# Idle TensorE products at the seams of a two-stage kernel, and one projection step to a tile

## The chip, the cores and the metric

The kernel runs on one core of a Trainium2 chip. The metric is the device time of one execution in microseconds (us). All data are float32. The core has five queues that work side by side: TensorE (PE) for matrix products, VectorE (DVE), ScalarE (ACT), GpSimd (POOL) and SyncE (SP), which here only starts transfers. A matrix product writes to PSUM, from where VectorE or ScalarE takes it. PEld is the loading of TensorE's stationary operand.

## The reference

Two computations follow each other. The first is a bidirectional recurrence over 4 batches, 1024 steps and 1024 channels: with a decay d per channel, `a[t] = a[t-1] * d + exp(k[t]) * v[t]` and `b[t] = b[t-1] * d + exp(k[t])`, forward and backward; the result x is `sigmoid(r)` times the ratio of the two sums, times a gain per batch.

The second repeats a block twice (NB = 2) on x, with S = 16 slots, K = 4 and 16 heads:

- `logits = rms(x) @ compete_w.T + compete_b`; for each slot the best four rows, with softmax weights
- `written` = the weighted sum of those four rows of `x @ write_w.T + write_b`; `ws = rms(ws + written)`
- q from x, keys and values from ws; attention of each row over the 16 slots; `x = rms(x + ctx @ out_proj_w.T + out_proj_b)`

The output is the input x plus the result.

## The kernel before

**Recurrence (to about 413 us).** The channels lie on partitions, so 32 tiles (i = 0 to 31: four batches, eight tiles of 128 channels) of 128 x 1024 are worked through, one per turn of a Python loop. Everything is emitted in a fixed program order (`pin` keeps an instruction in its place on its engine), and work on tile i is interleaved with the ends of tiles i - 1 and i - 2. VectorE does four scans per tile (`both`, L315), and three elementwise operations. ScalarE does the exponentials, one sigmoid over four tiles each time i % 4 is 0 (HK = 4; L274, with a table load before and behind it), the copies of transposed tiles, and the small `edges` values (L327) that the backward scans begin with. TensorE adds terms (`num`, L365), contracts a tile into the first block's logits (`raw`, L437), and transposes tiles (`ptr`, L451) to rows, which ScalarE sends to memory (`rows`).

Between these the loop places the steps of the list `projection`. They prepare `wo_cw`, the product of the output weights with the slots' competition weights, which the first block needs to get the second block's logits. `turn_weights(j, h)` transposes half of one 128-row tile of the output weights on TensorE (`pwt`, L483) and copies it back with ScalarE (L484); `group_products(j)` multiplies it in groups of four channel tiles (`acc`, L490, copied at L498); `group_sums` adds the groups (`pc`, L504, L508). There are 8 x 3 + 1 = 25 steps. All of them, and the transposes of tiles, share one PSUM bank, `ptr`, so each step waits for the copy of the one before.

SP issues the loads in program order: `kf` (the tile to come), `gate`, the output weights `wp` in four pieces from i = 2 on, write weights and key and value weights ahead of the first block (`load_ahead`), and the stores `turned_rows`. The pieces of weights share nine buffers (`wide`), so key and value pieces 1 to 4 take those of `wp` and wait for `group_sums`.

**Seam 1 (about 413 to 467 us).** After the last tile, its halves are finished, the logits are normalised, the last two tiles are transposed (`turn_ptr`, `turn_columns`, `turn`, L692) and copied out (L698). Then `write_slots(blk)` begins: VectorE finds each slot's four best rows; TensorE brings their numbers into two columns (`token_ps`, L769), GpSimd gathers the rows (L779), a second such product brings the weights (`share_ps`); then `pmix` (L807) forms the weighted sums, `pw` (L825) multiplies by the write weights, `pkv` (L875) by key and value weights, `pk` and `pv` fold the query and output weights into maps.

**Attention (twice 32 tiles of 128 rows).** `run` does, per tile, `psc` (scores, L1085), softmax, `pet` (transposes), `po` (output, L1142) and the norm. In the first block it also makes the second block's logits: `poc` (L1158), scaled, transposed by `turn_logits` (`lg`, L1227). Seam 2 (about 762 to 791 us) lies between the blocks: the last `lg`, top four, token, gather, the transposes of the first two row tiles (`ptr`, L1073, in `early`), `pmix` and `pw`.

## Time and profile before

| what | us |
|---|---|
| three timed runs | 1104.65, 1105.7, 1109.95 (median 1105.7) |
| the profiled execution | 1103.67, of which the span is 1101.9 |
| recurrence: one step, VectorE without a wait | 12.44 |
| first seam: pmix, pw | 7.06, 9.29 |
| second seam: pmix, pw | 3.84, 7.09 |
| mean granted clock of TensorE over the span | 0.945 of full |

The profile's page gives the busy share of each engine in 40 slices of the span (27.5 us each), the TensorE clock that was granted, and the chain of work that ended last. A timeline row reads: start, duration, engine, line and operation, what it writes and reads, the shape, how many, and in brackets the idle time of its engine before it and what ended it. Lines are those of the kernel before.

### The profile page before, as it was taken

The numbers are of one execution on the slowest core, as the hardware profiler recorded it, in microseconds if no ns is written. First come the engines' busy times: TensorE is split into PE (matmuls) and PEld (weight loads), VectorE is DVE, ScalarE is ACT, GpSimd is POOL, SyncE is SP. The second block draws the span as 40 slices with busy tenths as digits, with TensorE's granted clock in tenths as the row PEclk, the third lists the DMA queues.
The fourth block names the chain that finished last, engine by engine and source line by source line (L and its number), as shares of the span: only waits on it lengthen the run. The fifth ranks groups of instructions, "written<-read, shape, count | busy, mean of one in ns | idle before, by whom it ended". The sixth has DMA issues, their size and how long they took to land.

```text
span 1101.9 us, 11887 instructions
## 1 busy us (share of the span) xinstructions
PE 961.6 (87%) x4116; PEld 538.3 (49%) x4116; DVE 767.3 (70%) x1049; ACT 508.8 (46%) x791; POOL 546.3 (50%) x417
## 2 busy tenths in 40 slices
PE   2678787887878785899999999996899999999996
PEld 0223232322323232584666666664584676676763
DVE  7999999999999995144666666666234556555555
ACT  5475858667686753012344444444113333333332
POOL 4999889998999972100222222222100443434444
PEclk9798888999889898799999999999999999999999
DMA  8485564857564374590487778562770455555554
GB/s 270 144 295 157 168 188 138 277 160 248 153 214 132 93 243 114 204 396 21 172 294 261 262 259 294 183 222 92 282 285 21 160 192 197 196 196 205 191 210 153
DMA packets 121787, 218.78 MB, mean 199 GB/s; under 512 B 10928, under 2 KB 76592, under 8 KB 121728
## 3 DMA queue, kind: packets, MB, share of 16 engines
q1 hardware_dynamic: 87872, 199.15, 51.0%
q10 hardware_dynamic: 33280, 16.78, 5.3%
q0 software_dynamic: 576, 2.10, 0.6%
q8 instruction: 32, 0.52, 0.2%
q14 instruction: 27, 0.22, 0.1%
HBM read 150.90 MB, written 67.11 MB: 198 GB/s over the span
## 4 chain that ended last, share of the span: by engine, by line
PE 60%; DVE 24%; issue 5%; ACT 4%; POOL 3%; DMA 3%; SPq 1%; POOLq 0%; DVEq 0%; ACTq 0%
PE psc L1085 20%; PE po L1142 19%; DVE both L315 17%; DVE both L414 3%; PE pk L945 3%; PE pkv L875 3%; PE raw L437 2%; PE ptr L1073 2%; DVE ov L359 2%; PE pv L1013 2%; PE num L365 2%; PE pw L825 1%; PE pet L1131 1%; PE pmix L807 1%; PE poc L1158 1%
## 5 line engine op out<-in xcount | busy, mean ns | idle before, releaser
L1085 PE MATMUL psc<-km,xt 128*128 128x272 f32 (+1 forms) x1024 | 238.4, 386 | 0.0
L1142 PE MATMUL po<-vm,e 128*128 128x512 f32 x512 | 230.4, 593 | 0.9 <-ACT e L1132 0.9
L1085 PEld LDWEIGHTS psc<-km,xt 128*128 128x128 f32 x1024 | 189.5, 190 | 29.1
L365 PE MATMUL num<-ov,minus_ident 128*128 128x512 f32 x128 | 87.6, 821 | 96.1 <-DVE ov L359 96.1
L1119 POOL TENSOR_TENSOR e<-e,den 128x256 f32<-128x256 f32 x64 | 40.5, 633 | 253.7 <-DVE den L1117 232.2
L315 DVE TENSOR_TENSOR_SCAN both<-columns,edges,both 128x1024 f32<-128x1024 f32 x64 | 148.4, 2319 | 2.8 <-ACT edges L327 2.8
L1142 PEld LDWEIGHTS po<-vm,e 128*128 128x128 f32 x512 | 94.8, 190 | 95.7 <-issue 85.4
L1183 DVE SCALAR_TENSOR_TENSOR y<-y,inv,npost_bc 128x1024 f32<-128x1024 f32 x62 | 79.7, 1285 | 41.2 <-POOL inv L1178 41.2
L1151 DVE TENSOR_TENSOR y<-po,y 128x512 f32<-128x512 f32 x128 | 85.8, 674 | 30.4 <-PE po L1142 30.1
L1171 ACT ACTIVATE junk<-y 128x1024 f32<-128x1024 f32 x63 | 66.7, 1059 | 69.2 <-DVE y L1183 69.1
L365 PEld LDWEIGHTS num<-ov,minus_ident 128*128 128x128 f32 x128 | 27.6, 239 | 132.8 <-issue 68.4
L407 POOL TENSOR_TENSOR both<-both,quo 128x1024 f32<-128x1024 f32 (+1 forms) x33 | 75.7, 2293 | 20.4 <-ACT quo L394 19.7
L1178 POOL TENSOR_TENSOR inv<-mean,minus_half 128x1 f32<-128x1 f32 x64 | 35.5, 555 | 96.0 <-DVE mean L1176 96.0
L303 POOL TENSOR_TENSOR ekv<-ek,kf 128x1024 f32<-128x1024 f32 (+1 forms) x33 | 75.6, 2292 | 2.6
L1132 ACT COPY e<-pet 128x256 f32<-128x256 f32 x64 | 23.8, 372 | 112.8 <-PE pet L1131 112.7
L408 POOL TENSOR_TENSOR gate<-gate,quo 128x1024 f32<-128x1024 f32 (+1 forms) x33 | 75.4, 2284 | 0.0
L1280 POOL TENSOR_TENSOR y<-y,xin 128x1024 f32<-128x1024 f32 x31 | 73.2, 2361 | 1.4 <-DVE y L1183 1.4
L426 POOL TENSOR_TENSOR gate<-gate,both 128x1024 f32<-128x1024 f32 x31 | 73.3, 2363 | 1.2
L315 DVE TENSOR_TENSOR_SCAN both<-columns,ek 128x1024 f32<-128x1024 f32 (+1 forms) x32 | 71.5, 2234 | 2.4 <-POOL gate L426 2.4
L437 PE MATMUL raw<-gate,lhs 128*32 128x512 f32 x128 | 71.2, 681 | 0.6 <-POOL gate L426 0.6
L315 DVE TENSOR_TENSOR_SCAN both<-columns,ekv 128x1024 f32<-128x1024 f32 (+1 forms) x32 | 71.5, 2233 | 0.0
L1176 DVE TENSOR_SCALAR mean<-total 128x1 f32<-128x1 f32 x64 | 9.9, 154 | 85.4 <-ACT junk L1171 46.0
(195 smaller groups left out, 1522.5 us busy)
## 6 DMA issues: line engine op xcount, KB each, us to landing
y<-rows SPq DMA_DIRECT2D x64, 512.0 KB, 4.2
kf<-in_ft_dram SPq DMA_DIRECT2D x32, 512.0 KB, 5.2
gate<-in_xt_dram SPq DMA_DIRECT2D x32, 512.0 KB, 6.5
turned_rows<-gate SPq DMA_DIRECT2D x32, 512.0 KB, 3.5
xt<-turned_rows SPq DMA_DIRECT2D x32, 512.0 KB, 5.1
rows<-y SPq DMA_DIRECT2D x32, 512.0 KB, 3.0
xin<-in_x_dram SPq DMA_DIRECT2D x32, 512.0 KB, 4.5
rows<-stage ACTq DMA_DIRECT2D x31, 512.0 KB, 3.3
```

Source lines behind the costliest of these rows:

```text
L303: pin(nc.gpsimd.tensor_tensor(ekv[:, part], ek[:, part], kf[:, part], ALU.mult))
L315: nc.vector.tensor_tensor_scan(dst[:, way], dec, src[:, way], start, ALU.mult, ALU.add)
L365: nc.tensor.matmul(num_ps[:, ts(h, 512)], minus_ident, src[:, ts(h, 512)], start=first, stop=not first,)
L407: pin(nc.gpsimd.tensor_tensor(den, den, quo[:, part], ALU.mult))
L408: pin(nc.gpsimd.tensor_tensor(xk, xk, quo[:, part], ALU.mult))
L426: pin(engine.tensor_tensor(xk, xk, factor[:, part], ALU.mult))
L437: nc.tensor.matmul(raw[rows_b, ts(h, 512)], lhs[:, w].rearrange("p h s -> p (h s)"), src[:, ts(h, 512)], start=(k == 0 and w == k), stop=( ...
L1085: nc.tensor.matmul(psc[g][:, :n], xt_g[g][:, k, :], maps["km"][:, g // NT, k, :n], start=(k == 0), stop=(k == NK - 1),)
L1142: nc.tensor.matmul(po, et[:, ts(c, P)], vm[:, c, ts(h, 512)], start=(c == 0), stop=(c == 1),)
L1151: pin(nc.vector.tensor_add(half, po, half))
L1183: pin(nc.vector.scalar_tensor_tensor(y[g], y[g], inv[g], npost_bc, ALU.mult, ALU.mult))
L1280: pin(nc.gpsimd.tensor_add(y[g - 1], y[g - 1], xin[g - 1]))
```

## The change

It adds a helper, `hold_clock(bank, n)`, which emits n products of the identity with the first 512 columns of `npost_bc`, a constant, into a PSUM bank that nobody reads. They are placed: 7 behind the last copies of the recurrence (in the bank `ptr`), 5 in the first block and 1 in the second ahead of `pmix` (behind `early`), 4 in the first block's last turn behind `turn_logits` of the last tile but one, and 3 at the start of the second block's top four, ahead of token.

It also changes the projection. `group_products` now does two 128-row tiles in one step, with 16 products and one copy, so there are 16 + 4 + 1 = 21 steps in place of 25. One is taken in every tile with i % 4 not 0, from i = 3 on; before, it was 0, 1, 1, 2 for i % 4 = 0 to 3, from i = 5 on. The last is taken at i = 30 (before: 29). The four loads of `wp` are issued at i = 1 to 4 in place of 2 to 5, and of the last four loads of key and value weights, two each at i = 30 and 31 before, all stand at i = 31.

```diff
+    def hold_clock(bank, n):
+
+        for _ in range(n):
+            pin(nc.tensor.matmul(bank, ident, npost_bc[:, :512], start=True, stop=True))
...
-        def group_products(j):
-            acc = rec_ps.tile([P, 4, P], F32, tag="ptr", bufs=1, name=f"acc_{j}")[:, 0, :]
-            for o in (0, 2, 4, 6, 1, 3, 5, 7):
-                pin(
-                    nc.tensor.matmul(
-                        acc[ts(o // 2, 2 * S), :],
-                        cw_pad[:, o, :],
-                        weight_rows(j)[:, ts(o, P)],
-                        start=(o % 2 == 0),
-                        stop=(o % 2 == 1),
-                    )
-                )
-            pin(nc.scalar.copy(weight_rows(j)[:, :P], acc))
+        def group_products(j2):
+            acc = rec_ps.tile([P, 4, P], F32, tag="ptr", bufs=1, name=f"acc_{j2}")
+            for n in range(2):
+                for o in (0, 2, 4, 6, 1, 3, 5, 7):
+                    pin(
+                        nc.tensor.matmul(
+                            acc[ts(o // 2, 2 * S), n, :],
+                            cw_pad[:, o, :],
+                            weight_rows(2 * j2 + n)[:, ts(o, P)],
+                            start=(o % 2 == 0),
+                            stop=(o % 2 == 1),
+                        )
+                    )
+            pin(nc.scalar.copy(wo_next[j2][:, :, :P], acc[:, :2, :]))
...
-        for j in range(NJ):
-            for h in range(2):
-                projection.append(lambda j=j, h=h: turn_weights(j, h))
-            projection.append(lambda j=j: group_products(j))
+        for j2 in range(NJ // 2):
+            for n in range(4):
+                projection.append(lambda j=2 * j2 + n // 2, h=n % 2: turn_weights(j, h))
+            projection.append(lambda j2=j2: group_products(j2))
...
-            if 2 <= i < 6:
-                wo_next.append(load_rows(wo, i - 2, f"wp{i - 2}"))
+            if 1 <= i < 5:
+                wo_next.append(load_rows(wo, i - 1, f"wp{i - 1}"))
...
-            if i >= N - 2:
-                for n in range(2):
-                    load_ahead(0, 5 + 2 * (i - N + 2) + n)
+            if i == N - 1:
+                for n in range(5, 9):
+                    load_ahead(0, n)
...
-            for _ in range(min((0, 1, 1, 2)[i % HK], len(projection)) if i > HK else 0):
+            if i >= 3 and i % HK and projection:
                 projection.pop(0)()
...
             send(j, stage)
+        hold_clock(rec_ps.tile([P, 512], F32, tag="ptr", bufs=1, name="idle"), 7)
     rc_stack.close()
...
+        if last:
+            hold_clock(bank("po", "idle_topk"), 3)
         token = small_tile([P, 2], "token", U32)
...
         early()
+        hold_clock(bank("po", f"idle_rows{blk}"), 5 if first else 1)
...
                     turn_logits(g - 1)
+                    if here and not next_:
+                        hold_clock(bank("po", "idle_norm"), 4)
```

## The prediction

> **What bounds the kernel now.** I read the page's 40 slices first, then the chain in order of time, then TensorE's timeline at the two seams, the granted clock by stretches, and VectorE's idle times in the recurrence.

> ```profile
> PE 2678787887878785899999999996899999999996
> DVE  7999999999999995144666666666234556555555
> PEclk9798888999889898799999999999999999999999
> ```

> Three stages. Up to 413 us VectorE is full and steps follow each other every 12.44 us: only what makes VectorE wait counts there. From 467 us on, apart from the stretch around slice 28, TensorE is full at full clock. Between lie two seams in which neither is full; at the first (slices 15 to 17) the clock is low as well. TensorE's timeline there:

> ```profile
> 428.75 1.04 PE L692 MATMUL turn<-ident,gate 128*128 128x128 f32 x8
> 436.86 0.38 PE L769 MATMUL token_ps<-at,pick 128*64 128x2 f32 x4 [7.07 <-DVE neg L758]
> 437.99 0.38 PE L769 MATMUL share_ps<-wgt,pick 128*64 128x2 f32 x4 [0.75 <-DVE wgt L787]
> 443.76 7.06 PE L807 MATMUL pmix<-spare,spare 128*128 128x64 f32 x32 [5.40 <-DMA spare<-in_wb_dram]
> 451.28 9.29 PE L825 MATMUL pw<-ww,mix_t 128*64 128x512 f32 x32 [0.46 <-ACT mix_t L815]
> ```

> and at the second seam, between the blocks, the same work:

> ```profile
> 762.03 0.51 PE L1158 MATMUL poc<-vmc,e 128*128 128x16 f32 x4
> 764.02 0.28 PE L1227 MATMUL lg<-ident,lgs 128*16 128x128 f32 x1 [1.47 <-DVE lgs L1216]
> 768.36 0.38 PE L1227 MATMUL lg<-ident,lgs 128*16 128x128 f32 x1 [4.07 <-DVE lgs L1216]
> 772.04 0.38 PE L769 MATMUL token_ps<-at,pick 128*64 128x2 f32 x4 [3.30 <-DVE neg L758]
> 773.66 3.43 PE L1073 MATMUL ptr<-ident,y 128*128 128x128 f32 x16 [0.17 <-DMA y<-rows]
> 777.54 3.84 PE L807 MATMUL pmix<-spare,spare 128*128 128x64 f32 x32 [0.46 <-DMA spare<-rows,token]
> 781.85 7.09 PE L825 MATMUL pw<-ww,mix_t 128*64 128x512 f32 x32 [0.46 <-ACT mix_t L815]
> ```

> Equal products, 16.35 us at the first seam and 10.93 at the second; both stand on the chain. The clock says why (columns: stretch, its length, then busy us of PE, PEld, DVE, ACT, POOL, and the granted clock):

> ```profile
> 66.63:70.04 3.41, 1.51 (x4) 0.22 (x2) 3.38 (x3) 3.41 (x1) 3.33 (x3) 1.00 1.03 423
> 428.45:431.85 3.40, 1.33 (x13) 1.10 (x11) 3.15 (x6) 2.91 (x5) 0.00 (x0) 1.00 0.01 2
> 431.87:443.70 11.83, 0.76 (x8) 0.65 (x8) 5.58 (x15) 1.46 (x4) 4.97 (x6) 0.50 0.68 193
> 443.76:450.80 7.04, 7.04 (x32) 6.87 (x32) 0.00 (x0) 0.00 (x0) 0.00 (x0) 0.50 0.15 54
> 773.20:776.60 3.40, 3.23 (x18) 2.79 (x19) 0.45 (x2) 1.17 (x2) 3.10 (x4) 0.50 1.00 367
> ```

> The clock changes on a grid of 3.41 us in this trace. A stretch in which TensorE was busy 1.33 us (0.39) is followed by half clock; after one of 1.51 us (0.44) it stayed. It rose after 3.23 us of transposes (773.2 to 776.6), so the second seam reached pmix at full clock, and at the first seam only after a full stretch of pw: pmix, busy without a break for 7 us, did not raise it. At full clock 128x512 records follow each other at 0.43 us (eight po records in 3.43 us of the chain), so one 128x512 f32 product, two records, is 0.86 us, and 1.71 at half clock.

> In the recurrence VectorE waited four times for ScalarE's edge values, in two of the steps that hold the sigmoid:

> ```profile
> 117.59 2.35 DVE L315 TENSOR_TENSOR_SCAN both<-columns,edges,both 128x1024 f32<-128x1024 f32 x1 [0.62 <-ACT edges L327]
> 124.13 2.35 DVE L315 TENSOR_TENSOR_SCAN both<-columns,edges,both 128x1024 f32<-128x1024 f32 x1 [0.60 <-ACT edges L327]
> 169.24 2.35 DVE L315 TENSOR_TENSOR_SCAN both<-columns,edges,both 128x1024 f32<-128x1024 f32 x1 [1.01 <-ACT edges L327]
> 175.78 2.35 DVE L315 TENSOR_TENSOR_SCAN both<-columns,edges,both 128x1024 f32<-128x1024 f32 x1 [0.60 <-ACT edges L327]
> ```

> 2.83 us in all. The chain leads back from each pair through ScalarE's queue to two projection steps taken one after the other (i = 7 and 11), behind products that ran at half clock.

> **First seam: 7 + 5 idle products.** The 7 write the bank of turn_ptr, so they wait for ScalarE's copy of it (430.80 + 0.57), start at 431.4 and take 7 x 0.86 = 6.0 us, to 437.4. TensorE's token product behind them was ready at 436.86 and also waits for the last of them: +0.6 us. Behind token stand the cast, GpSimd's gather issue (438.40) and, 5.2 us later, pmix: take the 0.6 in full. The slots and bias loads on SP wait for the transposes, not for the idle products, and keep their time. The 5 (4.3 us) follow share at 439.0 and end at 443.3, before the gather's landing (443.76 + 0.6): cost nothing; without that cover each would cost 0.86. Gain: the gap in which the clock fell is now 1.6 us (429.8 to 431.4), so any 3.41 us there hold about 1.8 us of products (0.53, above 0.44): the clock stays. pmix becomes 3.84 (-3.2) and pw 7.09 (-2.2), as at the second seam; the gather's second half landed 2.1 us after the first, no later than a 3.84 us pmix needs it (1.9). Sum: -5.4 + 0.6 = **-4.8 us**. The weight loads behind pw are released by pw itself and move with it.

> [...]

> **Second seam: 4 + 3 + 1 products.** The 4 follow the lg transpose at 764.3 and end at 767.7, before 768.36; the 3 run 768.75 to 771.3, before token at 772.04; the one stands behind the row transposes, ahead of pmix. At full clock all are hidden. These transposes take 2.1 us instead of 3.43, but pmix waits for the gather (777.41), so nothing is won on the profiled execution. If a grid stretch spans the pause of 771.3 to 773.7 the clock falls once more and the last product ends up to 0.8 us after the gather. Between 0 and +0.8: **+0.3**, as that takes about half of the grid's positions. [...] The trace shows 1.00 after 3.4 us of transposes, so I count nothing; but other executions, whose grid lies otherwise, may well start pmix cold. [...]

> **Recurrence: 21 steps.** Removed: the second step in each i % 4 = 3, and eight groups of acc products with eight copies (four of double width take their place). At i = 7 an acc (0.73 of TensorE) and its copy (0.27) leave the queue ahead of the sigmoid: -1.1 of 1.22. At i = 11 a turn (0.60) and its copy (0.59): -1.2 of 1.61. Step i = 3 gets a turn that was not there (0.66 + 0.59): at i = 16, behind two steps, VectorE did not wait, so free. A double group is about 1.2 us of TensorE, no more than a turn with its copy. group_sums (1.96 us) moves from i = 29 to 30, into TensorE's pause of 2.36 us before 400.26; its copy (0.27) precedes a quo that waits until 400.34 anyway. SP: the four output-weight loads go one step earlier, the first ahead of the store at 37.77 into SP's pause from 25 us; two of the four key/value loads move behind the store of i = 29, to 403 us, and behind group_sums. They are done by about 414 us, pkv reads them at 462, and the row stores start at 431.9: free. No POOL instruction moves. **-2.2**, between -2.8 and +2: the grid decides in which steps TensorE is late.

> Sum: -4.8 + 0.3 - 2.2 = -6.7 on the profiled execution (1103.67 us, of which the span is 1101.9): **1097.0 us**. That execution is 2.0 below the median of the runs (1105.7), so against the median it is -8.7, or 0.8%.

> **Rivals.** A: the clock holds over the idle products and falls in pmix, because the 0.8 us pause before it plus a pmix that counts half fall into one stretch. For: pmix did not raise the clock. Against: the second seam's pmix followed a 0.46 us pause without a fall. It costs about 3 us (half of pmix and of one stretch of pw): 1100.0. B: the clock falls before the 7 products, they start cold for up to two stretches (four at 1.71), end at 440.8, and token is 3.9 late: net -1.5 at the seam, 1100.3; with the recurrence unimproved 1102.5. C, slower: the idle products do not raise or hold the clock at all. Then 7 take 12 us (token +6.6), 5 take 8.6 and end 9.8 us after pmix's old start; 4 and 3 at the second seam hold token up by 4.6 more, and the seams gain nothing: 1103.7 + 14.4 - 2.2 = 1115.9. It decides from the second cold product on token's path (0.6 + 2 x 0.86 exceeds the 2.2 of the recurrence). Against: one stretch of pw, with the same 512 columns, raised the clock at 455.7. D: the change does not do what it says: the clock holds but pmix waits for the gather or its loads, and only the recurrence changes: -2.2 + 0.6 + 0.3 gives 1102.4. Against: pmix ran in 3.84 us at the second seam with its gather landing 1.9 us apart.

> **Numbers.** Main 0.63 (1094.5 to 1099.5), A 0.17, B 0.12, C 0.04, D 0.04. Range 1094.0 to 1103.0 leaves out C and B's tail. 0.5%, about what a measurement of this kernel can tell from no change, is 5.5 us: faster below 1100.2. Main and 0.11 of A and B, which end at about that bound, give 0.74, C 0.04, the rest 0.22.

> **What would show it.** Right: granted clock 1.00 from 425 us on through pmix and pw; pmix 3.8 and pw 7.1 at both seams; token at 437.5 or less than 0.7 later than before relative to the transposes; VectorE's waits for edges under 1.5 us in total. Wrong: 0.50 within 431 to 455 us, an idle product longer than 0.86 us apart, or new VectorE waits in the steps i = 4, 8, 12.

## The result, and the profile after

The changed kernel takes 1097.2 us in the median of five runs (1096.5 to 1097.7), beside 1105.2 us of the kernel before: ratio 0.9919, 95% interval 0.9898 to 0.994. Run again beside the experiments it gave 0.9923 (0.9901 to 0.9945). Its profiled execution has 1097.41 us, a span of 1095.6, against 1101.9 before: 6.3 us less. A gain of 8 us in the medians was forecast as 8.7, and 6.3 in the profiled executions as 6.7. The sum holds. Of its three terms, the experiments below bear out the first, contradict the second and leave the third open.

First the 40 slices of the changed kernel:

```profile
PE   2688788877878788899999999998999999999996
DVE  7999999999999995144666666656144555555555
PEclk9789899989989899999999999999999999999999
```

Nothing below 9 is left in the clock from slice 16 on. At the first seam (slices 15 to 17) TensorE is warm, that is, at full clock. At the second (slices 28 and 29) one cold stretch of 3.4 us hides within slice 29; it is shown below. TensorE's timeline at the first seam:

```profile
429.29 6.28 PE L115 MATMUL idle<-npost_bc,ident 128*128 128x512 f32 x14 [1.63 <-ACT stage L704]
435.67 0.28 PE L776 MATMUL token_ps<-at,pick 128*64 128x2 f32 x4
436.92 4.56 PE L115 MATMUL idle_rows<-npost_bc,ident 128*128 128x512 f32 x10
443.23 3.76 PE L817 MATMUL pmix<-spare,spare 128*128 128x64 f32 x32 [1.75 <-POOL bias_rows L808]
447.45 7.09 PE L835 MATMUL pw<-ww,mix_t 128*64 128x512 f32 x32 [0.46 <-ACT mix_t L825]
```

pmix and pw are 10.85 us in place of 16.35. Token has lost its wait for VectorE (7.07 us before): it now stands directly behind the 7 products, which end last. At the second seam:

```profile
757.81 3.60 PE L115 MATMUL idle_norm<-npost_bc,ident 128*128 128x512 f32 x8
762.14 2.74 PE L115 MATMUL idle_topk<-npost_bc,ident 128*128 128x512 f32 x6
765.61 0.28 PE L776 MATMUL token_ps<-at,pick 128*64 128x2 f32 x4 [0.73 <-DVE neg L765]
766.86 3.30 PE L1083 MATMUL ptr<-ident,y 128*128 128x128 f32 x16
771.36 3.76 PE L817 MATMUL pmix<-spare,spare 128*128 128x64 f32 x32
775.58 7.09 PE L835 MATMUL pw<-ww,mix_t 128*64 128x512 f32 x32 [0.46 <-ACT mix_t L825]
```

Here pmix and pw are as long as they were in the profile before. Token to pmix is 5.75 us against 5.50: the +0.3 of the forecast. The 3 products end before token is ready (it waits 0.73 us for neg), so they are hidden. The 4 and the 3 do not keep the clock up, though (columns as in the forecast: stretch, length, busy us of PE, PEld, DVE, ACT, POOL, clock, DMA share, GB/s):

```profile
763.99:767.41 3.42, 1.94 (x16) 1.04 (x15) 2.54 (x9) 0.39 (x2) 1.02 (x1) 1.00 0.93 351
767.41:770.82 3.41, 3.41 (x15) 2.52 (x13) 0.05 (x2) 2.34 (x4) 2.82 (x4) 0.50 0.99 356
```

After a stretch that was busy for 0.57 the clock is at half for one stretch, in which the row transposes run (3.30 us, and not the 2.1 of the forecast). They and the one product behind them fill it (3.41 us), and the clock is at 1.00 again from 770.82 us on, ahead of pmix at 771.36.

In VectorE's waits of the recurrence the edges (2.8 us before) are gone. One wait has grown, at the end of the recurrence, and the stretch of granted clock beside it says why. The wait before, then after:

```profile
418.03 0.76 DVE L414 SCALAR_TENSOR_TENSOR num<-both,twice_root,num 128x512 f32<-128x512 f32 x1 [2.54 <-POOL both L407]
415.90 0.76 DVE L419 SCALAR_TENSOR_TENSOR num<-both,twice_root,num 128x512 f32<-128x512 f32 x1 [3.99 <-PE num L370]
```

```profile
405.59:409.01 3.42, 0.61 (x2) 0.00 (x0) 3.39 (x4) 0.89 (x2) 1.63 (x2) 1.00 1.02 387
409.01:412.42 3.41, 2.96 (x4) 1.41 (x5) 2.87 (x3) 2.91 (x4) 3.41 (x3) 0.50 1.05 402
439.73:443.14 3.41, 1.75 (x5) 0.44 (x3) 0.00 (x0) 0.00 (x0) 2.62 (x4) 1.00 0.98 308
443.14:446.55 3.41, 3.32 (x30) 3.35 (x31) 0.00 (x0) 0.00 (x0) 0.00 (x0) 1.00 0.06 24
```

TensorE had 0.61 us of work in one stretch and ran its last numerator at half clock in the next: VectorE waits 3.99 us there instead of 2.54. The last two lines are the seam: 1.75 us of idle products, then pmix, all at 1.00.

The difference of the two profiled executions, by the end of the turn transposes, the start of pmix and the start of pkv:

| part | before | after | difference | forecast |
|---|---|---|---|---|
| recurrence, to the last turn transpose | 429.79 | 427.66 | -2.1 | -2.2 |
| from there to token | 7.07 | 8.01 | +0.9 | +0.6 |
| token to pmix | 6.90 | 7.56 | +0.7 | 0 |
| pmix to pkv (first seam) | 18.78 | 13.27 | -5.5 | -5.4 |
| token to pmix (second seam) | 5.50 | 5.75 | +0.25 | +0.3 |

The rows add to -5.8 of the 6.3 us. From this table alone the forecast looks right in kind at every term. It compares one execution with one.

### The profile page after: what moved, and what is told of

Its sections match the earlier page's. It is cut to its first block, busy times and chain, and to the rows that moved or that the text cites. A ratio compares the mean times of both kernels' runs of the same rounds, so it can differ in the third digit from the quotient of the medians.

```text
span 1095.6 us, 11962 instructions
## 1 busy us (share of the span) xinstructions
PE 972.7 (89%) x4156; PEld 541.9 (49%) x4156; DVE 767.0 (70%) x1049; ACT 507.5 (46%) x787; POOL 546.4 (50%) x417
## 4 chain that ended last, share of the span: by engine, by line
PE 58%; DVE 31%; issue 4%; POOL 3%; ACT 2%; DMA 1%; SPq 0%; POOLq 0%; DVEq 0%; ACTq 0%
DVE both L320 22%; PE psc L1095 20%; PE po L1152 19%; DVE both L419 3%; DVE ov L364 3%; PE ptr L1083 3%; PE pk L955 3%; PE pkv L885 3%; PE pv L1023 2%; PE pet L1141 1%; PE pw L835 1%; PE raw L442 1%; PE poc L1168 1%; PE num L370 1%; PE pmix L817 1%
```

## The experiments

All ratios are to the kernel before, timed on the same chip beside the kernel in question; its medians there were 1107.5, 1106.5 and 1106.4 us. One thousandth is 1.1 us.

**Either half alone.** The first kernel is the changed one with all `hold_clock` calls taken out:

```
-        hold_clock(rec_ps.tile([P, 512], F32, tag="ptr", bufs=1, name="idle"), 7)
...
-            hold_clock(bank("po", "idle_topk"), 3)
...
-        hold_clock(bank("po", f"idle_rows{blk}"), 5 if first else 1)
...
-                        hold_clock(bank("po", "idle_norm"), 4)
```

> The changed kernel with none of the idle products: only the 21 projection steps and the moved weight loads. Theory: the two halves of the change add up, and this half brings the recurrence's 2.1 us alone (turn transposes end at 427.7 instead of 429.8), while the clock falls at both places as before: pmix 7.0 and pw 9.3 at the first seam, so about 1102 to 1103.5, ratio 0.998. Rival 1: the steps bring most of the 8 us, by moving the stretches in which the clock is judged so that it no longer falls: then about 1098, with pmix 3.8 at the first seam. Rival 2: the saving of the steps is lost again in the last stage's cold stretch: 1105, no change.

Measured: 1105.9 us, ratio 0.9994 (0.9978 to 1.001): -0.7 us, between -2.4 and +1.1. Its profile shows no wait for edges and pmix at 7.06 us.

The second has the idle products at all places and the 25 steps and weight loads of the kernel before (the cut is against the changed kernel, and leaves out `group_products` and the loads at i = 30 and 31):

```
-            if i >= 3 and i % HK and projection:
+            for _ in range(min((0, 1, 1, 2)[i % HK], len(projection)) if i > HK else 0):
                 projection.pop(0)()
...
-            if 1 <= i < 5:
-                wo_next.append(load_rows(wo, i - 1, f"wp{i - 1}"))
+            if 2 <= i < 6:
+                wo_next.append(load_rows(wo, i - 2, f"wp{i - 2}"))
```

> The kernel before with the idle products at all their places (7, 5, 4, 3, 1) and its own 25 projection steps and loads. Theory: -5.5 from pmix and pw, +1.6 for the later token and gather, +0.3 at the second seam: -3.6 to -4.2, about 1101, with pmix 3.8 and pw 7.1 at the first seam and VectorE's four waits for edges (2.8 us) still there. Rival 1 (the products bring nothing alone): 1105. Rival 2 (they bring nearly all, since the steps' saving would be hidden behind the seam): 1098.

Measured: 1096.9 us, ratio 0.9923 (0.9902 to 0.9943), as much as the whole change. Rival 2 is right about the size: the idle products carry all of the gain that can be measured. Its reason, that the steps' saving would be hidden, was not tested. Nor did the waits for edges come back with the 25 steps. In this profile only three steps are longer than the 12.44 us of the others, by about 0.2 us each, against 2.83 us in the profile before. In the changed kernel's second profile, with 21 steps, one wait of 0.41 us stands. So those waits differ from execution to execution: the profile before showed an execution with many. In the twelve profiles with 21 steps they come to 0.9 us at most in any one; only two profiles have 25 steps, one with 2.8 us and one with none.

**The change again.** The changed kernel was timed once more beside the kernels that follow.

> The changed kernel itself, beside these. Theory: its times lie close together (within 1.5 us), since both seams are warm in every execution, and 8 to 10 us below the kernel before, whose executions spread over 7 us. Rival: its spread is that of the kernel before, with a median near 1099.

Measured: 1098.5 us (1095.4 to 1099.9), ratio 0.9923 (0.9901 to 0.9945). The difference holds; the forecast of its spread does not, 4.5 us instead of 1.5. The kernel before, beside it, spread from 1100.8 to 1111.8. So the change has taken away a part of what differs between executions, not all.

**Either seam alone.** The changed kernel without the 4, 3 and 1:

```
-        if last:
-            hold_clock(bank("po", "idle_topk"), 3)
...
-        hold_clock(bank("po", f"idle_rows{blk}"), 5 if first else 1)
+        if first:
+            hold_clock(bank("po", f"idle_rows{blk}"), 5)
...
-                    if here and not next_:
-                        hold_clock(bank("po", "idle_norm"), 4)
```

> The changed kernel without the 4, 3 and 1 products at the second seam; the 7 and 5 at the first stay. Theory: they are hidden and bought nothing on the profiled grid: TensorE falls to half clock near 764 to 767 us in both, the row transposes then run 3.4 us at half clock and raise the clock before pmix; 1097 within 0.7, ratio to the changed kernel 1.000. Rival (insurance: the grid of the clock lies otherwise from run to run or after the earlier changes): pmix starts at half clock and pmix and pw take 16.3 instead of 10.9 us: about 1102.

Measured: 1101.0 us (1097.0 to 1107.5), ratio 0.9949 (0.9928 to 0.997). Its profiled execution took 1107.54 us, and its second seam (timeline) shows what the profile before did not:

```profile
776.87 7.06 PE L816 MATMUL pmix<-spare,spare 128*128 128x64 f32 x32 [0.96 <-DMA spare<-rows,token]
784.39 8.39 PE L834 MATMUL pw<-ww,mix_t 128*64 128x512 f32 x32 [0.46 <-ACT mix_t L824]
```

15.45 us in place of 10.85. The row transposes ran here too, at half clock, but the stretch in which most of them fell held 2.50 us of work (0.73), and the clock did not rise. The insurance rival is right: without products the second seam was warm in one execution and cold in another, and the grid of stretches lay otherwise in the two: the transposes began 0.46 us after the start of a stretch in the profile before (773.66 and 773.20), and 1.26 us ahead of one here (772.15 and 773.41). Of the three profiles without them, two reached pmix warm after 10.2 us at half clock (the kernel before and the steps alone) and this one stayed cold for 23.9 us. In the eleven profiles with the 4, 3 and 1 the cold part is one stretch of 3.4 us in ten, with pmix warm in each (3.68 to 3.94 us), and two stretches in one. Which of the 4, the 3 and the 1 earns this was not tested.

This execution is long for a second reason. It lost the clock at the first seam as well, with the 7 and the 5 in place:

```profile
441.99 6.76 PE L816 MATMUL pmix<-spare,spare 128*128 128x64 f32 x32 [1.98 <-issue]
449.21 8.73 PE L834 MATMUL pw<-ww,mix_t 128*64 128x512 f32 x32 [0.46 <-ACT mix_t L824]
```

Here pmix began 1.98 us after the end of the 5, and pmix and pw lost 4.6 us, as much as at the second seam. So of the 10.1 us between this execution and that of the profile after, the two seams hold 9.2, in equal parts.

And the changed kernel without the 7 and the 5:

```
-        hold_clock(rec_ps.tile([P, 512], F32, tag="ptr", bufs=1, name="idle"), 7)
...
-        hold_clock(bank("po", f"idle_rows{blk}"), 5 if first else 1)
+        if last:
+            hold_clock(bank("po", f"idle_rows{blk}"), 1)
```

> The changed kernel without the 7 and the 5 products; the 4, 3 and 1 at the second seam stay. Theory now: each seam's products are worth what its cold pmix and pw cost where they are cold, and the two add: the first seam -5.5 +1.5 = -4, the second 0 to -5.5 by the execution, in the median -3 to -4; so 4 us above the changed kernel, about 1101 to 1102, with pmix 7.0 and pw 9.3 at the first seam. Rival: the first seam's cold clock is hidden behind the weight loads after it (wkv, wq) and its products bring less than 1.5: 1098.

Measured: 1102.8 us, ratio 0.9971 (0.9957 to 0.9985), pmix 7.06 and pw 8.82 at the first seam. Against the changed kernel (0.9921, the mean of its two ratios) the first seam's products are worth 0.0050, 5.5 us (3 to 8, if the intervals of the ratios are combined), and the second seam's 0.0028, 3.1 us (0 to 6). Together that is 8.6 of the whole's 8.7: they add, and the middle values leave nothing for the steps.

**Which products of the first seam.** Without the 7, and without the 5:

```
only_five:   -        hold_clock(rec_ps.tile([P, 512], F32, tag="ptr", bufs=1, name="idle"), 7)
only_seven:  -        hold_clock(bank("po", f"idle_rows{blk}"), 5 if first else 1)
             +        if last:
             +            hold_clock(bank("po", f"idle_rows{blk}"), 1)
```

> The changed kernel without the 7 products at the end of the recurrence; the 5 ahead of pmix stay. Theory A (the 5 alone warm the clock): token comes 0.9 us earlier, the 5 start at half clock (1.7 us each) and the clock rises after one or two stretches of 3.4 us, so they end within 1 us of the gathered rows; pmix and pw at full clock or nearly: 1096 to 1098. Theory B (7 are needed): the 5 are still at half clock when they end, pmix does not raise it, and the seam is as without products, with 2 us of the 5 on top: 1102 to 1104.

> The changed kernel without the 5 products ahead of pmix; the 7 stay. Theory: TensorE then stands still for 7 us between share and pmix, the clock falls there, pmix 7.0 and pw 9.3 as before and the token is 0.9 us late on top: 1101.5 to 1103, worse than without both. Rival: the clock holds from the 7 through the pause: 1097.

Measured: with the 5 alone 1098.4 us, ratio 0.9929 (0.9907 to 0.9951), the same as the whole change; with the 7 alone 1103.3, ratio 0.9972 (0.9954 to 0.999), as without either, with pmix at 7.06. The five alone, in the timeline and by stretches:

```profile
434.59 6.23 PE L115 MATMUL idle_rows<-npost_bc,ident 128*128 128x512 f32 x10
440.65 3.99 PE L816 MATMUL pmix<-spare,spare 128*128 128x64 f32 x32
```

```profile
434.57:437.98 3.41, 3.41 (x6) 1.52 (x5) 0.42 (x2) 0.00 (x0) 2.99 (x3) 0.50 0.61 169
437.98:441.40 3.42, 3.42 (x15) 1.89 (x13) 0.00 (x0) 0.00 (x0) 1.97 (x4) 1.00 0.87 280
```

They start at half clock, fill one stretch, and the clock is at 1.00 in the next. Token stands 7.07 us behind the transposes again, as before the change. The 7 hold a clock that the 5 bring back here anyway, and cost token 0.9 us. This execution's grid suits the five exactly, and it is the fastest of its six; that they always warm in time isn't shown (the runs reach from 1095.3 to 1099.8).

**Five in place of seven.**

```
-        hold_clock(rec_ps.tile([P, 512], F32, tag="ptr", bufs=1, name="idle"), 7)
+        hold_clock(rec_ps.tile([P, 512], F32, tag="ptr", bufs=1, name="idle"), 5)
```

> The changed kernel with 5 products instead of 7 at the end of the recurrence (they end 1.7 us earlier, at 433.9 instead of 435.6; token's input is ready at 434.7). Theory: token starts 0.9 us earlier and everything behind it too, if the pause between the 5 and token (0.9 us) does not let the clock fall: -0.9, about 1096.3. Rival 1: pmix starts when its gathered rows land, and they land late since they share the DMA queues with the slots and wb loads, which keep their time: no more than -0.3, about 1097. Rival 2: the pause makes the clock fall at token: pmix at half clock, up to +5.4, 1102.6.

Measured: 1097.5 us (1096.0 to 1101.1), ratio 0.9918 (0.9897 to 0.9938), the same as the change. Token is back at 7.08 us behind the transposes and pmix 7.07 behind token, so the 0.9 us is the products' doing. That the rows land late because they share queues with the other loads isn't borne out: token to pmix is 6.7 to 7.8 us in all profiles but that of the narrow products below, early token or late. In its profiled execution (1101.09 us) rival A of the prediction happened: pmix took 4.90 us and pw 9.26, 3.3 us more than warm (the forecast said 3). The stretch ahead of the fall:

```profile
442.77:446.19 3.42, 2.86 (x24) 2.79 (x25) 0.00 (x0) 0.00 (x0) 0.18 (x1) 1.00 0.43 139
```

TensorE was busy for 0.84 of it, all with pmix's products of 64 columns, and the clock fell to 0.50 in the next. That led to the next test.

**Busy time, or columns.** The five products of 512 columns become 38 of 64:

```
-            pin(nc.tensor.matmul(bank, ident, npost_bc[:, :512], start=True, stop=True))
+            pin(nc.tensor.matmul(bank[:, :c], ident, npost_bc[:, :c], start=True, stop=True))
...
-        hold_clock(bank("po", f"idle_rows{blk}"), 5 if first else 1)
+        if first:
+            hold_clock(bank("po", "idle_rows0"), 38, 64)
+        else:
+            hold_clock(bank("po", f"idle_rows{blk}"), 1)
```

> The changed kernel with the 5 products of 512 columns ahead of pmix replaced by 38 of 64 columns, which keep TensorE busy for about as long (pmix needs 0.117 us each: 4.5 us). Theory: what holds the clock is the columns that pass, not the busy time: these count as pmix does, half or less, the clock falls before pmix, which then takes 7.0 us and pw over 8: 1101.5 to 1103, as without the 5. Rival: busy time holds it: 1097 to 1098.5, pmix 3.8.

Measured: 1102.2 us (1098.0 to 1110.9), ratio 0.9973 (0.9947 to 0.9999). The time is no clean answer, since the products were mis-sized: each is two records, 0.11 us apiece at full clock, so 38 would keep TensorE busy for 8.5 us and not 4.5, and hold pmix up by themselves. The twelve executions fall into two groups, eight from 1098.0 to 1102.6 us and four from 1109.9 to 1110.9. The profiled one (1110.7 us) is one of the four:

```profile
436.40 13.98 PE L115 MATMUL idle_rows<-npost_bc,ident 128*128 128x64 f32 x76
```

```profile
435.75:439.16 3.41, 2.98 (x29) 2.99 (x29) 0.71 (x4) 0.00 (x0) 2.28 (x3) 1.00 0.48 112
442.58:445.99 3.41, 3.41 (x18) 3.41 (x17) 0.00 (x0) 0.00 (x0) 0.00 (x0) 0.50 0.05 19
445.99:449.40 3.41, 3.41 (x18) 3.41 (x17) 0.00 (x0) 0.00 (x0) 0.00 (x0) 0.50 0.00 0
```

After a stretch that was busy to 0.87 the clock fell, and in the following stretches, busy without a break, it stayed at 0.50 (to 452.82 us), and pmix behind them took 7.04 us. So narrow products did not raise the clock here. Whether they held it went with how many fell into the stretch: here 25 began in the one ahead of the fall, while pmix's, 30 in a stretch, held it alone in the changed kernel (443.14 to 446.55). The eight faster executions have no profile; probably the clock held in them.

**Toward a better version.** Three more products in TensorE's pause ahead of the last numerator; 6 and 7 in place of 7 and 5 at the first seam; and both of these with one more product ahead of the 16-column pboc products in the first block, behind which the clock fell for a stretch in the second profile of the changed kernel (it followed 492.3 to 495.7 us, in which TensorE was busy for 0.81; pv after it took 1.7 us longer):

```
tail_three:  +            if i == N - 1:
             +                hold_clock(rec_ps.tile([P, 512], F32, tag="ptr", bufs=1, name="idle_last"), 3)
                          add_negated(num_ps[i], ov, True)
six_seven:   -        hold_clock(rec_ps.tile([P, 512], F32, tag="ptr", bufs=1, name="idle"), 7)
             +        hold_clock(rec_ps.tile([P, 512], F32, tag="ptr", bufs=1, name="idle"), 6)
             -        hold_clock(bank("po", f"idle_rows{blk}"), 5 if first else 1)
             +        hold_clock(bank("po", f"idle_rows{blk}"), 7 if first else 1)
all_three:   both, and
                                  pb = bank("aux", "pboc", 1)
             +                    hold_clock(pb, 1)
```

> The changed kernel with 3 more products in TensorE's pause ahead of the last numerator (405.9 to 409.4 us). Theory: where the clock falls at about 409 (the changed kernel's profile: VectorE then waits 3.99 us for the last num in place of 2.54), it no longer does: -1.4 in those executions, about -0.7 to -1 in the median: 1096.5 to 1097.5, and the wait is 2.5 in the profile. Rival: the wait is set by VectorE's and GpSimd's own work: no change, 1098.

> The changed kernel with 6 products in place of 7 at the end of the recurrence and 7 in place of 5 ahead of pmix. Theory: token starts 0.6 to 0.8 us earlier, and the longer row ahead of pmix leaves no pause in which the clock could fall: -0.7 in the median and no pmix over 4 us: 1097 to 1097.8. Rival: the 7 end after the gathered rows have landed and hold pmix up by what token won: 1098.3.

> The changed kernel with the two edits above (3 products ahead of the last numerator; 6 and 7 at the first seam) and one more product ahead of the 16-column pboc products, behind which the clock fell for one stretch in some executions (pv 4.95 instead of 3.27 us). Theory: these are the places where executions still differ; the three bring 0.8 + 0.7 + (0.8 - 0.3) = 2 us in the median and leave a spread under 2 us: about 1096. Rival: one product there costs 0.9 on a full TensorE and the others bring nothing: 1098.5 to 1099.

Measured: 1099.8 us, ratio 0.9946 (0.9927 to 0.9965), for the three at the tail. They did not help. In this execution TensorE's last raw products ended 1.4 us later than in the changed kernel's profile (407.6 against 406.2), and the idle ones were still running when the last ov was ready:

```profile
407.56 2.84 PE L115 MATMUL idle_last<-npost_bc,ident 128*128 128x512 f32 x6
410.24 1.88 PE L370 MATMUL num<-ov,minus_ident 128*128 128x512 f32 x4
```

VectorE then waited 3.35 us for num, better than 3.99 but worse than the 2.54 of executions whose clock holds anyway. In the profile of all three together the same products cost nothing (2.54). An idle product is free only in a pause that is always there.

Six and seven gave 1097.0 us (1095.2 to 1098.5), ratio 0.9915 (0.9898 to 0.9933): as fast as the change, with the lowest ratio of all, but the intervals overlap, so no gain over it is shown. Its profile has the shortest span of all (1093.4 us), with token 0.85 us nearer to the transposes than in the change and pmix at 3.79. All three together gave 1097.7 (1095.4 to 1103.6), ratio 0.993 (0.9904 to 0.9956): no gain, and the spread is not gone. Its profile shows where the spread still comes from, at the second seam:

```profile
766.97:770.38 3.41, 2.29 (x18) 1.77 (x16) 0.00 (x0) 0.32 (x1) 0.39 (x1) 1.00 0.48 183
```

```profile
768.64 5.47 PE L819 MATMUL pmix<-spare,spare 128*128 128x64 f32 x32 [1.12 <-DMA spare<-rows,token]
```

Here the gathered rows came 1.1 us after the one product ahead of pmix was done. That pause and the beginning of pmix fell into one stretch (busy 0.67), and the clock fell in pmix. More products at that place weren't tried, nor was six and seven with the single product ahead of pboc alone.

## Why the prediction was right, and where it was not

**The total** was right: 1097.0 forecast, 1097.2 measured. That it came so close is in part luck. The forecast for the profiled execution, -6.7, was set against the median of the runs, which gave another -2.0 that no term explains. A gain at the second seam, which the forecast put at +0.3, and a recurrence that brings less than the -2.2 then cancelled.

**First seam, -4.8.** Right in kind and nearly in size. In the profile pmix and pw brought 5.5, as forecast. Token's term was mis-sized: +0.6 forecast, 0.94 measured, the same in all profiles with the 7 (8.01 us behind the transposes against 7.07). The 7 x 0.86 left out that the last record runs on beyond its 0.43 us (6.28 us from the first start to the last end of 14 records that start 0.43 apart) and that token starts 0.1 us after it. To pmix the loss against the profile before was 0.8 to 1.8 us; the rest varies between executions with the time from token to pmix. Net -3.9 in the profiled pair, 5.5 in the ratios. What the forecast didn't ask is whether the 7 are needed. With the 5 alone the time is the same within the intervals: in its profile the clock went from 0.50 to 1.00 behind the stretch that they filled.

**Second seam, +0.3.** This step failed. It was costed on the profiled execution, where the seam was warm already. The prediction said that other executions "may well start pmix cold", and then counted nothing for them. By the ratios the products there bring 3.1 us (0 to 6), since they cut the cold part of the seam from 10 us or more to one stretch of 3.4 us in ten of eleven profiles. That the profiled execution lay 2 us below the median of its runs may have the same cause; the forecast only noted it. Against the median, a gain at this seam belonged in the sum. The +0.25 of the profiled pair came as described: the clock fell once more, and the last product ended just ahead of pmix.

**Recurrence, -2.2.** This step isn't borne out, although the profiled pair shows -2.1. The steps alone bring -0.7 us, between -2.4 and +1.1, and with the products in place the 25 steps are as good as the 21. The four waits were read as the price of two projection steps in a row. With 21 steps they are indeed gone, but with 25 steps another execution had no such wait either, only 0.6 us of longer steps in place of 2.83. So they come and go between executions, and the 2.83 was taken for what every execution pays; that TensorE's clock is their cause was argued from the chain and not tested. "The grid decides in which steps TensorE is late" stood in the range and should have stood in the value. The whole of the 2 us isn't excluded by the interval. (In the working, 0.73 and 0.27 make 1.0 and not 1.1; the -2.2 is right with the 1.0.) A loss that was not foreseen stands beside it: in some executions TensorE loses its clock before the last numerator (3.99 us of waiting instead of 2.54). It isn't tied to the change, since it shows in kernels with 21 steps and with 25.

**Unbroken work and transposes.** In the profile of the narrow products several stretches of 3.41 us of unbroken busy time stayed at 0.50, as pmix's 7.04 us did in the profile before. The forecast took the second seam for warm because the clock had risen over transposes once (773.20 to 776.60 us of the profile before, busy 3.23). It did so again in the profile of five in place of seven, after a stretch in which only transposes ran (770.45 to 773.87 us, busy 3.35; pmix behind it took 3.76 us). After the 2.50 us of work without the second seam's products it did not. The two differ in the amount of work in the stretch (the last section counts it), and to count the seam as warm was not safe.

**Rivals.** A happens, at the place that was named: of the seven profiles with the 5 wide products ahead of pmix, two lose the clock in pmix, five in place of seven (3.3 us) and the one without the second seam's products (4.6 us). With 7 products there, neither of two does. B's cold start is harmless in the one profile that has it, the five alone, where pmix and pw are warm. C, that idle products neither raise nor hold the clock, is false for 512 columns: the five alone were followed by 1.00 after 0.50, and the changed kernel's kept 1.00 from 429 us to pmix. With 64 columns they did not raise it, and did not hold it in the profiled execution (0.50 from 439.16 us on). D is false: pmix and pw are warm and the gain is there.

**The marks.** Clock 1.00 from 425 us through pw, pmix 3.8 and pw 7.1, waits for edges under 1.5 us, and products 0.43 us a record all came out. Token under 0.7 us late did not.

## What to carry to other kernels

In these profiles the granted clock changed on a grid of 3.41 us that lay otherwise from execution to execution. Pmix began at 443.23 us in the changed kernel's profile and in that of five in place of seven; a stretch began at 443.14 in the one and at 442.77 in the other, and only in the other did the clock fall in pmix. So one profile shows one draw: count the columns that pass in each stretch, cost a change on the stretches that could go either way, and take the distance of the profiled execution from the median as a hint of what that draw left out. To hold the clock over a seam like this one, put wide products directly ahead of the work that must be warm (the 5 of 512 columns ahead of pmix alone: 1098.4 us), rather than far ahead on the path of a small product that would have to wait for them (the 7 alone: 1103.3 us, and token 0.9 us later). Count on them as free only in a pause that every execution has.

## What the runs showed of the hardware

In these profiles the busy share of a stretch does not tell what the clock did after it: at full clock it held after 0.51 and fell after 0.87. Records of 512 columns started 0.43 us apart at full clock, which is 0.84 ns a column. Records of pmix and of the narrow idle products (64 columns) and of pboc (16 columns) all started 0.11 us apart there; at 0.84 ns a column, 64 columns take 0.05 us of that and 16 columns 0.01 us. The table counts the columns that pass in a stretch of 3.41 us. It is an estimate from the trace: each record's columns are laid from its start, at 0.84 ns each at full clock and 1.68 ns at half, and records that overlap are counted once. (after_again is the second profile of the changed kernel, no_second_seam the kernel without the 4, 3 and 1.)

| stretch | clock in it | busy | columns | clock after it |
|---|---|---|---|---|
| after_again 492.26, pv and pboc | full | 0.81 | 1090 | half |
| all_three 766.97, a pause and pmix | full | 0.67 | 1460 | half |
| five_first 442.77, pmix | full | 0.84 | 1560 | half |
| narrow_rows 435.75 | full | 0.87 | 1570 | half |
| after 443.14, pmix | full | 0.97 | 1920 | full |
| after 439.73, idle products | full | 0.51 | 1890 | full |
| before 445.51, pmix | half | 1.00 | 1020 | half |
| narrow_rows 442.58 | half | 1.00 | 1020 | half |
| no_second_seam 773.41, transposes | half | 0.73 | 1320 | half |
| before 773.20, transposes | half | 0.95 | 1680 | full |
| only_five 434.57, 512 columns | half | 1.00 | 1930 | full |
